# One exp in twenty-four moved from ScalarE to VectorE in a graph attention kernel

## The chip, the cores and the metric

The kernel runs on one core of a Trainium2 chip. The metric is the device time in microseconds of one launch, taken as the median of three runs. A core has five engines that run side by side, each through its own list of instructions in order: TensorE (PE, with its weight loads PEld), VectorE (DVE), ScalarE (ACT), GpSimd (POOL), and SyncE (SP), which here only issues DMAs. They wait for each other by semaphores.

## The reference

Four layers on a graph of N = 3327 nodes with 128 features, x of shape (3327, 128) and a dense fp32 matrix adj of (3327, 3327). Nearly all time goes into layer 0, an attention with 128 heads of only 8 features, whose logits get adj added twice:

```python
q = (x @ Wq.T).reshape(d, n, h)      # d = 128 heads, n = 3327, h = 8; k and v alike
a = jnp.einsum('dnh,dmh->dnm', q, k) * scale
a = a + spatial_encoding + edge_encoding          # both are adj
a = jax.nn.softmax(a, axis=2)
out = jnp.einsum('dnm,dmh->dnh', a, v).reshape(n, h * d)
return out @ Wo.T
```

Each of the four layers ends as x = layernorm(x + layer(x, adj)). Layers 1 to 3 are products of adj, or its transpose, with 128 columns. The attention needs 128 x 3327 x 3327, some 1.4 billion, exps.

## The kernel before

A prologue makes q, k and v, splits q and k into a high and a low part in fp32r, and writes them to scratch tensors in HBM (`q_s`, `k_s`, `v_img`). Then `attention()` runs, then the four layers' remaining products. There is also a path for large logits, `wide_attention()`, that these inputs don't take.

**Blocks, groups, sets.** The attention loop goes over 28 blocks: seven pieces of CW = 476 query columns times four ranges of keys (KBS), two of seven 128-key tiles and two of six. In a block it goes through 128 heads in 32 groups of GROUP = 4. For each head, `exponents(b, d, si)` works on three sets of tiles, one after the other: 3, 2 and 2 tiles where the block has seven, 2, 2 and 2 where it has six (`SETS`). For a set, TensorE adds this head's q·k to PSUM (L544): the PSUM tiles `sc` keep running logits, adj included, from head to head. That is possible since the keys hold the previous head's rows beside this head's, with negated queries, so that one product takes the old head's logits away and adds the new ones. A tile uses 64 of TensorE's rows, and tiles alternate between its two halves of rows, so two run side by side. Then one ScalarE instruction takes the exp of the whole set, from `sc` to `e` in SBUF (L548). There is one `sc` per set: the logits of a set for the next head wait until the exp of this set has been read. So TensorE can be at most two exps ahead.

**Weighs.** The exps of a group are multiplied with its values one group later. `weigh(b, g, r)` does it for one key tile and the four heads, four matmuls side by side into PSUM bank `o` (L562); a group has as many weighs as tiles, seven or six. [...] Three groups (PACK) share `o`: the first weigh of a pack restarts the bank, and after the last weigh of a pack, or of a block, `flush` adds the bank into `acc` on VectorE (L572, L574).

**The order.** Within the loop the order of TensorE, ScalarE, GpSimd and VectorE instructions is that of the program (`manual_schedule`). A group has 12 places, one after each set of each head; `PLACES` says after which places a weigh is issued:

```python
PLACES = {7: (1, 2, 4, 6, 7, 9, 11), 6: (1, 3, 5, 7, 9, 11)}
```

**Loads and side work.** At the first head of group n, `prepare` has SP load keys and queries for group n+2 (`load_heads`, L426 and L431, three buffers) and the values of group n+1 (`load_values`, L478), which GpSimd spreads into `v_pad` (L481). At the second head VectorE copies the keys of group n+1 one head on (`copy_keys`, L458 and L460), at the third it makes the negated and doubled queries (`copy_queries`, L466, L468, L469), at the fourth it does one step of `background_work`: adj is transposed and its row and column sums are taken in 78 pieces, spread over the groups (`PACE`), for the later layers; GpSimd issues the pieces' stores (L217).

## Time and profile before

| What | us |
|---|---|
| Median of three runs (11,215.2 to 11,219.94) | 11,218.06 |
| The profiled execution, its own time | 11,220.65 |
| Its span, first to last instruction | 11,218.9 |
| PE busy | 10,904.3 (97%) |
| ScalarE busy | 10,122.0 (90%) |
| VectorE busy | 5,422.6 (48%) |
| GpSimd busy | 1,712.0 (15%) |
| Exps on ScalarE (L548), 10,752 of them | 9,933.0 |
| VectorE's key copies (L458, L460) | 652.7 + 1,706.2 |
| VectorE's query copies (L466, L468, L469) | 807.9 + 353.8 + 1,034.9 |

The profile is one execution recorded by the hardware. A row of a group of instructions gives its line in the kernel, engine, operation, what it writes and reads, the count, the busy time with the mean ns of one, and the idle time of the engine just before with what ended it ("<-"). In the order in time, a row begins with the start and the length in us. A record of one instruction can overlap with the next of the same engine, so that records can be longer than the pace at which they follow; and a busy PE may be one whose records wait.

### The profile page before, as it was taken

The page shows a single profiled execution, that of the slowest core. Times are in us where ns is not written, and L with a number is a line of the kernel's source. Part 1 is how long each engine was busy: PE and PEld are TensorE (multiplying, and loading weights), DVE is VectorE, ACT ScalarE, POOL GpSimd, SP SyncE. Part 2 cuts the span into 40 slices and gives each one's busy share as a digit, 9 for nine tenths or more (in the row PEclk, how much of TensorE's full clock was granted, in tenths as well). Part 3 has the DMA queues.
Part 4 walks back from the last instruction along what each step waited for, and adds up shares of the span by engine and source line. Part 5 has one row for each costly group of instructions (what it writes and reads, how often), then busy time and mean ns, then how long its engine had stood idle before and what let it go on. Part 6 is the DMA issues. An engine that isn't in the chain of part 4 may idle for free. (4 is left out here: it accounts for less than half of the span.)

```text
span 11218.9 us, 197557 instructions
## 1 busy us (share of the span) xinstructions
PE 10904.3 (97%) x76607; PEld 3924.3 (35%) x76607; DVE 5422.6 (48%) x7864; ACT 10122.0 (90%) x11194; POOL 1712.0 (15%) x2738
## 2 busy tenths in 40 slices
PE   6699999999999999999999999999999999999999
PEld 2233333333333333333333333333333333333779
DVE  6444555445554455544555445554444544444312
ACT  2499999999999999999999999999999999999400
POOL 3311112111221111211112111121110100001200
PEclk8799999999999999999999999999999999999999
DMA  8655555555655556555556555555555555555686
GB/s 290 172 82 82 87 93 94 78 86 87 92 95 79 85 88 91 96 78 86 86 91 97 79 87 83 85 86 81 81 78 78 78 79 75 74 74 78 186 284 246
DMA packets 769475, 1157.40 MB, mean 103 GB/s; under 512 B 152703, under 2 KB 636401, under 8 KB 754201
## 3 DMA queue, kind: packets, MB, share of 16 engines
q1 hardware_dynamic: 673994, 913.64, 51.0%
q0 software_dynamic: 82432, 128.80, 4.4%
q10 hardware_dynamic: 12110, 102.22, 2.6%
q8 instruction: 616, 10.09, 0.5%
q14 instruction: 323, 2.65, 0.1%
HBM read 999.98 MB, written 143.98 MB: 102 GB/s over the span
## 5 line engine op out<-in xcount | busy, mean ns | idle before, releaser
L548 ACT ACTIVATE e<-sc 128x952 f32<-128x952 f32 (+1 forms) x10752 | 9933.0, 1350 | 93.9 <-PE sc L544 70.1
L562 PE MATMUL o<-e,v_pad 128*32 128x476 f32 (+1 forms) x46592 | 5867.7, 575 | 15.0 <-DVE acc L574 1.6
L544 PE MATMUL sc<-qt,kt 64*128 64x476 f32 x23296 | 4789.2, 458 | 58.0 <-DVE qt L468 3.8
L544 PEld LDWEIGHTS sc<-qt,kt 64*128 64x128 f32 x23296 | 2172.3, 183 | 5252.0 <-ACT e L548 5174.1
L460 DVE CAST kt<-kt 32x1152 fp32r<-32x1152 f32 (+1 forms) x1792 | 1706.2, 952 | 1358.2 <-DMA kt<-k_s 1352.2
L481 POOL COPY v_pad<-vs 128x192 f32<-128x192 f32 (+1 forms) x896 | 439.1, 490 | 8402.8 <-DMA vs<-v_img 6324.9
L562 PEld LDWEIGHTS o<-e,v_pad 128*32 128x32 f32 (+1 forms) x46592 | 922.8, 108 | 1538.9 <-issue 1536.1
L574 DVE TENSOR_TENSOR acc<-o,acc 128x476 f32<-128x476 f32 x231 | 151.0, 654 | 2373.6 <-PE o L562 2373.6
L469 DVE CAST qt<-qt 64x1904 fp32r<-64x1904 f32 x896 | 1034.9, 1155 | 30.5
L217 POOL DMA_DIRECT2D adjT_s<-at x1352 | 816.5, 612 | 213.4 <-DMA adjT_s<-at 77.6
L466 DVE TENSOR_SCALAR qt<-qt 32x1428 fp32r<-32x1428 f32 x896 | 807.9, 902 | 12.5
L458 DVE CAST kt<-kt 32x512 fp32r<-32x512 f32 (+1 forms) x1736 | 652.7, 376 | 38.2 <-PE sc L544 2.8
L572 DVE COPY acc<-o 128x476 f32<-128x476 f32 x77 | 50.3, 654 | 934.6 <-PE o L562 934.6
L1001 PE MATMUL bank<-y,eT 128*128 128x128 f32 (+1 forms) x4056 | 473.9, 276 | 0.4 <-DVE h L1123 0.4
L1001 PEld LDWEIGHTS bank<-y,eT 128*128 128x128 f32 (+1 forms) x4056 | 465.3, 192 | 5.7 <-DVE h L1123 0.6
L468 DVE TENSOR_SCALAR qt<-qt 32x476 fp32r<-32x476 f32 x896 | 353.8, 395 | 0.9
L966 ACT ACTIVATE rstd<-mv,eps 128x1 f32<-128x1 f32 x104 | 30.6, 295 | 302.5 <-DVE mv L964 291.5
L581 POOL DMA_DIRECT2D o_s<-acc x308 | 283.8, 926 | 41.4 <-DVE acc L574 23.6
L323 ACT ACTIVATE hi<-pp 128x1024 fp32r<-128x1024 f32 x52 | 52.8, 1025 | 178.5 <-PE pp L274 150.1
L274 PE MATMUL pp<-wqT,xT 128*128 128x512 f32 x104 | 61.7, 727 | 87.6 <-DVE lo L324 87.1
L1104 PE MATMUL bank<-a,y 128*128 128x512 f32 (+2 forms) x364 | 145.5, 562 | 0.0
L439 DVE MEMSET qt<- 32x476 f32 x28 | 12.7, 455 | 261.3 <-PE sc L544 260.4
(143 smaller groups left out, 1954.8 us busy)
## 6 DMA issues: line engine op xcount, KB each, us to landing
kt<-k_s SPq DMA_DIRECT2D x2688, 96.0 KB
kt<-k_s SPq DMA_DIRECT2D x896, 128.0 KB
qt<-q_s SPq DMA_DIRECT2D x896, 119.0 KB
qt<-q_s SPq DMA_DIRECT2D x1792, 59.5 KB
eT<-adjT_s SPq DMA_DIRECT2D x39, 1664.0 KB
eT<-adjT_s ACTq DMA_DIRECT2D x39, 1664.0 KB
vs<-v_img SPq DMA_DIRECT2D x448, 112.0 KB
adjT_s<-at POOLq DMA_DIRECT2D x1352, 32.0 KB, 3.8
```

Source lines behind the costliest of these rows:

```text
L217: nc.gpsimd.dma_start(out=flat_ap(adjT_s, (t * P + 32 * q) * NP + c * PIECE, [[NP, 32], [P, ns], [1, P]]), in_=at[32 * i:32 * i + 32].rear ...
L458: nc.vector.tensor_copy(kt[64 * rg + 32:64 * rg + 64, 0, 0:ns[rg] * P], heads[b, g - 1][0].bitcast(F32)[64 * rg:64 * rg + 32, GROUP - 1, 0 ...
L460: nc.vector.tensor_copy(kt[64 * rg + 32:64 * rg + 64, 1:, 0:ns[rg] * P], kf[64 * rg:64 * rg + 32, 0:GROUP - 1, 0:ns[rg] * P])
L466: nc.vector.tensor_scalar(qt[32:64, 1:], qf[0:32, 0:GROUP - 1], -1.0, None, ALU.mult)
L468: nc.vector.tensor_scalar(qt[32:64, 0], before, -1.0, None, ALU.mult)
L469: nc.vector.tensor_copy(qt[64:128], qf[0:64])
L481: nc.gpsimd.tensor_copy(vp[:, 32:32 + nt * GROUP * 32].rearrange("p (x c) -> p x c", c=32)[:, :, 0:H], vs[:, 0:nt * 32].rearrange("p (x c) ...
L544: nc.tensor.matmul(s[:, i, 0:CW], lhsT=kt[64 * rg:64 * rg + 64, k, pos * P:(pos + 1) * P], rhs=qt[64 * rg:64 * rg + 64, k, :], start=False ...
L548: nc.scalar.activation(e[:, 0:n, :], s[:, 0:n, 0:CW], AF.Exp, scale=2.0)
L562: nc.tensor.matmul(o[32 * j:32 * j + 32, 0:CW], lhsT=values[b, g][:m, c:c + 32], rhs=es[b, g * GROUP + j, r][:m, :], start=(r == 0 and u = ...
L581: nc.gpsimd.dma_start(out=flat_ap(o_s, blocks[b][0] + (f * PACK * GROUP + j) * N, [[GROUP * N, nb], [SLOTS, A1], [1, CW]]), in_=acc[32 * j ...
L1001: nc.tensor.matmul(ps[:n, 0:D], lhsT=e[:m, s, :n], rhs=y[:m, s, col:col + D], start=(s == 0), stop=(s == T - 1))
```

## The change

In every second group (those with even number), the exp of the third set of the group's first head is no longer a ScalarE instruction. `vector_exp` computes it on VectorE from nine instructions on 128x952 elements. The first one reads `sc` and so frees it; the other eight stand in a list `vec`, from which the loop emits one ahead of each following place. The polynomial gives the exp times a constant, so all other exps get the matching `bias=shift`, a [128,1] tile, where they had none. The lines below are those of the changed kernel.

Further: VectorE's key copies are gone, and the keys are loaded a second time into the rows that they filled. The values are loaded once for two groups. The places of the weighs differ between groups of odd and even number (in each pair, the first tuple is that of odd groups), and two weighs may share a place. The side work on adj has one buffer in place of two (`pe2`), a period of 8 groups in place of 9, and is done in two bursts, at groups 3 and 5 of the period.

```diff
-PACE = 9
+PACE = 8
+SHIFT = 6.625
+POLY = (-7.292605475782272, 41.836134677209586, -181.05570822282746, 522.4277799178005, -753.7042669615115)
+ROUND = 1.5 * 2 ** 23 + 127 + 256
...
+    shift = const.tile([P, 1], F32, name="shift")
+    nc.gpsimd.memset(shift, SHIFT)
...
-                tc.tile_pool(name="pe2", bufs=2) as pe, \
+                tc.tile_pool(name="pe2", bufs=1) as pe, \
...
-            PLACES = {7: (1, 2, 4, 6, 7, 9, 11), 6: (1, 3, 5, 7, 9, 11)}
+            PLACES = {7: ((0, 2, 4, 4, 7, 7, 9), (0, 0, 4, 7, 7, 9, 10)),
+                      6: ((0, 2, 4, 5, 7, 9), (0, 0, 3, 6, 8, 10))}
...
-                for rg in range(2):
-                    for u in range(2):
-                        row = 64 * rg + 16 * u
-                        nc.sync.dma_start(
-                            out=kf[row:row + 16, :, 0:ns[rg] * P],
-                            in_=flat_ap(k_s, d * N + (k0 + (ns[0] if rg else 0)) * P,
-                                        [[RS, 16], [N, GROUP], [1, ns[rg] * P]]))
+                for back in range(2):
+                    j = 1 if back and g == 0 else 0
+                    for rg in range(2):
+                        for u in range(2):
+                            row = 64 * rg + 32 * back + 16 * u
+                            nc.sync.dma_start(
+                                out=kf[row:row + 16, j:, 0:ns[rg] * P],
+                                in_=flat_ap(k_s, (d + j - back) * N + (k0 + (ns[0] if rg else 0)) * P,
+                                            [[RS, 16], [N, GROUP - j], [1, ns[rg] * P]]))
...
-            def copy_keys(b, g):
...
-                vs = kq.tile([P, 7 * 32], F32, name="vs")
-                nc.sync.dma_start(out=vs[:, 0:nt * 32],
-                                  in_=flat_ap(v_img, k0 * HD + g * nt * 32, [[T * HD, P], [1, nt * 32]]))
+                if g % 2 == 0:
+                    pairs[b, g // 2] = kq.tile([P, 2, 7 * 32], F32, name="vs", bufs=2)
+                    nc.sync.dma_start(out=pairs[b, g // 2].rearrange("p a c -> p (a c)")[:, 0:2 * nt * 32],
+                                      in_=flat_ap(v_img, k0 * HD + g * nt * 32, [[T * HD, P], [1, 2 * nt * 32]]))
+                vs = pairs[b, g // 2].rearrange("p a c -> p (a c)")[:, g % 2 * nt * 32:(g % 2 + 1) * nt * 32]
...
                     worked.append((u, c, next(steps)))
+                    next(steps)
                     turning.append(steps)
-                elif turning:
-                    if next(turning[0], None) is None:
-                        turning.pop()
+                if n % PACE == 5 and turning:
+                    for _ in turning.pop():
+                        pass
...
-                elif n + 1 < len(groups):
-                    if d % GROUP == 1:
-                        copy_keys(*groups[n + 1])
-                    elif d % GROUP == 2:
-                        copy_queries(*groups[n + 1])
-                    else:
-                        background_work(n)
+                elif d % GROUP == 2 and n + 1 < len(groups):
+                    copy_queries(*groups[n + 1])
+                elif d % GROUP == 3:
+                    background_work(n)
+
+            vec = []
+
+            def vector_exp(e, x):
+                y = ex.tile([P, 2, CW], F32, name="ey")
+                t = ex.tile([P, 2, CW], F32, name="et")
+                ti = t.bitcast(I32)
+                nc.vector.tensor_scalar(y, x, -63 * math.log(2.0), 2 / math.log(2.0), ALU.max, ALU.mult)
+                vec.append(lambda: nc.vector.tensor_scalar(t, y, ROUND, None, ALU.add))
+                vec.append(lambda: nc.vector.scalar_tensor_tensor(y, t, ROUND, y, ALU.subtract, ALU.subtract))
+                vec.append(lambda: nc.vector.tensor_scalar(ti, ti, 23, None, ALU.logical_shift_left))
+                for i, a in enumerate(POLY):
+                    vec.append(lambda i=i, a=a: nc.vector.scalar_tensor_tensor(
+                        e, e if i else y, a, t if i == len(POLY) - 1 else y, ALU.add, ALU.mult))
...
-                nc.scalar.activation(e[:, 0:n, :], s[:, 0:n, 0:CW], AF.Exp, scale=2.0)
+                if (b * NHG + d // GROUP) % 2 == 0 and (d % GROUP, si) == (0, 2):
+                    vector_exp(e[:, 0:n, :], s[:, 0:n, 0:CW])
+                else:
+                    nc.scalar.activation(e[:, 0:n, :], s[:, 0:n, 0:CW], AF.Exp, bias=shift, scale=2.0)
...
-                copy_keys(*groups[0])
...
+                        if vec:
+                            vec.pop(0)()
                         exponents(b, d, si)
-                        if queue and place in PLACES[len(queue_of)]:
+                        for _ in range(PLACES[len(queue_of)][d // GROUP % 2 == 0].count(place) if queue else 0):
                             weigh(*queue.pop(0))
```

## The prediction

> **What bounds the kernel now.** I read the busy time by stretches of the span first, then the costliest groups, then the order in time. From 433 to 10,435 us the attention loop runs; ScalarE is never idle in it:

> ```profile
> 2000.00:4000.00 2000.00, 1984.88 (x14140) 633.79 (x14137) 1005.12 (x1388) 1987.41 (x2111) 328.60 (x550) 1.00 0.57 86
> ```

> The columns after the length are PE, PE's weight loads, VectorE, ScalarE (1987.41 of 2000), GpSimd, TensorE clock, DMA share. PE looks as full, but its records contain waiting; the groups say who waits:

> ```profile
> L548 ACT ACTIVATE e<-sc 128x952 f32<-128x952 f32 (+1 forms) x10752 | 9933.0, 1350 | 93.9 <-PE sc L544 70.1
> L544 PEld LDWEIGHTS sc<-qt,kt 64*128 64x128 f32 x23296 | 2172.3, 183 | 5252.0 <-ACT e L548 5174.1
> L574 DVE TENSOR_TENSOR acc<-o,acc 128x476 f32<-128x476 f32 x231 | 151.0, 654 | 2373.6 <-PE o L562 2373.6
> ```

> The exps (L548) idle 93.9 us in all; the logits' weight loads wait 5174 us for them. VectorE (48% busy) waits for PE, so its work is worth nothing by itself. The pace is read where the queries of each group are loaded, in a block of seven and one of six tiles:

> ```profile
> 5007.29 1.02 SPq L426 DMA_DIRECT2D qt<-q_s  x3
> 5019.19 1.02 SPq L426 DMA_DIRECT2D qt<-q_s  x3
> ...
> 5601.41 1.02 SPq L426 DMA_DIRECT2D qt<-q_s  x3
> 5611.70 1.02 SPq L426 DMA_DIRECT2D qt<-q_s  x3
> ```

> So a group of 12 exps takes 11.90 or 10.29 us: 0.857 us for an exp of 952, 1.26 for one of 1428 (eight and four of them in the first). PE is close behind:

> ```profile
> 5002.49 0.16 PEld L562 LDWEIGHTS o<-e,v_pad 128*32 128x32 f32 x8 [0.33 <-issue]
> 5003.43 0.19 PEld L544 LDWEIGHTS sc<-qt,kt 64*128 64x128 f32 x2 [0.78 <-ACT e L548]
> 5003.84 0.16 PEld L562 LDWEIGHTS o<-e,v_pad 128*32 128x32 f32 x8 [0.23 <-issue]
> ```

> From start to start a weigh takes PE 0.94 us and the logits of two tiles 0.41; three tiles, which need a second round through the two row halves, I take as 0.63. So PE could be little faster than ScalarE, and what stops PE for more than its lead of two exps stops ScalarE.

> [...] The exps before have none; after, every one has `bias=shift`. [...] with the same shape from PSUM with and without a pointer:

> ```profile
> L1044 ACT ACTIVATE y<-bank,dinv 128x128 f32<-128x128 f32 x25 | 9.3, 374 | 4.4 <-PE bank L986 4.4
> L1055 ACT COPY y<-bank 128x128 f32<-128x128 f32 x25 | 6.7, 267 | 60.4 <-DVE x L1054 60.4
> ```

> Does it stay when they follow each other? [...] a copy without a pointer hands over after 0.15 us, L1044 after 0.26.

> ```profile
> 10501.78 0.25 ACT L978 COPY xT<-bank 128x128 f32<-128x128 f32 x1
> 10501.93 0.37 ACT L1044 ACTIVATE y<-bank,dinv 128x128 f32<-128x128 f32 x1
> 10502.19 1.07 ACT L1027 COPY oT<-bank 128x512 f32<-128x512 f32 x2
> ```

> [...] L1084 has both in SBUF, L1123 one in PSUM.

> ```profile
> L466 DVE TENSOR_SCALAR qt<-qt 32x1428 fp32r<-32x1428 f32 x896 | 807.9, 902 | 12.5
> L324 DVE SCALAR_TENSOR_TENSOR lo<-pp,hi 128x1024 fp32r<-128x1024 f32 x52 | 62.7, 1218 | 30.6 <-ACT hi L323 26.4 <-DMA q_s<-lo 4.0
> L1084 DVE SCALAR_TENSOR_TENSOR h<-z,dinv,x 128x128 f32<-128x128 f32 x25 | 8.8, 352 | 0.9
> L1123 DVE SCALAR_TENSOR_TENSOR h<-bank,inv_row,z 128x128 f32<-128x128 f32 x25 | 8.8, 351 | 39.3 <-PE bank L1001 39.3
> ```

> **The change part by part.**
> *Exps taken from ScalarE:* 448 (one in each even group of 28 blocks x 16) x 0.857 = -384 us, all of it on the path that sets the end.
> *Bias pointer:* 10,304 exps left; [...] 0.116 (0.262 - 0.146 above), taken 0.10: +1030. The pace becomes 0.957 and 1.36.
> *The polynomial:* nine VectorE instructions on 128x952. From the rows [...]: 1.15 (PSUM) + 0.65 + 1.15 + 0.65 + 5 x 1.15 = 9.36 us. Each but one waits for the one before, and such a wait leaves a gap instead of an overlap:

> ```profile
> 5023.38 0.90 DVE L466 TENSOR_SCALAR qt<-qt 32x1428 fp32r<-32x1428 f32 x1
> 5024.20 0.39 DVE L468 TENSOR_SCALAR qt<-qt 32x476 fp32r<-32x476 f32 x1
> 5024.63 1.15 DVE L469 CAST qt<-qt 64x1904 fp32r<-64x1904 f32 x1
> ```

> L468 starts 0.08 before L466 ends, L469 (it waits for L468) 0.04 after. So 9.6 us; the query copies (5023.38 to 5025.78: 2.4) stand among them by program order. The total (VectorE about 5423 - 2359 + 4193 = 7256 us) has room.
> *What is queued behind it:* in an even group the weigh of place 10 is the last; if it ends a pack of three groups, `flush` follows on VectorE behind all nine. The next odd group's weigh at place 0 restarts bank `o` and waits for that flush; the logits of set 1 stand behind it on PE, and ScalarE behind those. Six times in a block (five packs and the block's last), 168 times in all. This is worked out on a clock with T0 = start of the even group's first exp, for seven tiles / six. Its queue is then: the group's first logits start at -1.5 (two exps ahead, less the 0.4 by which a record, 1.31 us for 952 elements in the groups by form, outlasts the pace), two weighs at place 0 end at +1.0 / +0.8, the logits of set 1 are ready at 1.45 / 1.3 (0.48 for one pair), where ScalarE wants it at 1.36 / 0.96 (bubble 0.1 / 0.3), the first VectorE operation starts at 1.7 / 1.5. Plus 9.6 + 2.4 + 0.7: flush ends at 14.4 / 14.2. The even group has 11 exps: the next starts at 12.25 / 10.8, so that PE wants to weigh at 11.35 / 9.7 (as the even group's weighs at -0.9 / -1.1) and waits 3.0 / 4.5; the odd group's first exp ends at 13.6 / 11.8. The odd group's set 1 is ready 1.5 us after the flush (weigh 0.94, logits 0.48, hand-over): 15.9 / 15.7. ScalarE idles 2.3 / 3.9, mean 3.1 x 168 = +520. Before, the flush at place 11 met an idle VectorE (L562's row on the page has PE waiting 1.6 us for L574 in all).
> *Bubble in even groups:* 224 x (0.1 + 0.3) = 90 at most, 0 at least if PE regains it; taken 45.
> *At nothing:* key copies gone (L460, L458: 2359 us, all beside ScalarE). Key loads doubled: eight issues for four, 1.7 us more on SP, which then idles about 9 us a group; the keys' share of the DMA time (382 of 914 MB of a queue at 51%: 21 points) comes twice, 0.58 to about 0.8, still hidden, as loads go out two groups (over 20 us) ahead; if late, the first logits of a group wait. Set 2's logits now wait for VectorE's first operation (1.15 us), but are wanted three places later. One value load for two: half the packets, GpSimd's copies as before. Single piece buffers, PACE 8: loads at 0, last reading at 5, stores at 6 of 8 groups; 78 x 8 = 624 of 896 groups. Its bursts on VectorE (two operations of 1.22 us) fall at the last head of odd groups, where no polynomial runs.
> Sum: -384 + 1030 + 520 + 45 = +1211 on the profiled 11,220.65, which is 2.6 above the median of three runs: **12,430 us**. Own range: bias -72/+165, chain 5% either way 100, bubble 45: 12,210 to 12,740.

> **Rivals.** (A) *The bias is read under the exp before.* For it: records of L548 overlap deeply (1.31 at a pace of 0.86). Against: L1044. Groups are then shorter and the flush later against them: ScalarE idles 3.4 / 5.0, 168 x 4.2 = 706, bubbles 110: -384 + 816 = +432, 11,650. (B) *The flush is ready in time*, because VectorE is quicker or PE later: -384 + 1030 + 45: 11,910. It decides from a chain 3 to 4.5 us shorter; the rows that price it (1.15 and 0.65 us) speak against that. (C) *ScalarE stays the only pace and an exp in 24 is gone*: place L548, price -384, bubbles 110 back: 10,945, faster. It decides if what is added to ScalarE's stream stays under 384/10,304 = 37 ns an exp and the flush under 384/168 = 2.3 us together; for it, ScalarE's idle 93.9 us; against, both numbers above. That the exps don't move is excluded by the program order.

> **Chances.** Main 0.72, A 0.11, B 0.09, C 0.08 (0.02 of it within 0.2%, about what a measurement of this kernel can tell from no change). Range 11,620 to 12,700: it leaves out C and the tails. Faster 0.06, same 0.02, slower 0.92.

> **What would show it.** L548's pace 0.95 in six-tile groups with a `shift` operand (0.86: A); the weighs' idle time put down to VectorE's `acc`, some 168 times and 3 to 4.5 us each (none: B); VectorE's polynomial rows 1.15 and 0.65 us; no wait of the logits for key loads. A shorter span would refute both terms at once.

## The result and the profile after

| | before | after |
|---|---|---|
| median, us | 11,217.0 | 12,624.1 (12,618.2 to 12,627.7) |
| ratio to before | | 1.1254, interval 1.1234 to 1.1273 |
| profiled span, us | 11,218.9 | 12,616.4 |
| first to last exp, us | 10,001.9 | 11,400.5 |

The kernel became slower by 12.5%, 1407 us. Of these, 1399 lie between the first and the last exp, so the stages around the attention loop can be left alone.

The costliest groups of instructions of the kernel after (count, then busy time and mean ns of one, then the engine's idle time ahead of them and what ended most of it):

```profile
L565 ACT ACTIVATE e<-sc,shift 128x952 f32<-128x952 f32 (+1 forms) x10304 | 10523.7, 1176 | 902.9 <-PE sc L558 862.1
L579 PE MATMUL o<-e,v_pad 128*32 128x476 f32 (+1 forms) x46592 | 5845.9, 592 | 671.3 <-DVE acc L591 529.7
L558 PEld LDWEIGHTS sc<-qt,kt 64*128 64x128 f32 x23296 | 2296.6, 188 | 5420.6 <-ACT e L565 4053.0
L534 DVE TENSOR_SCALAR ey<-sc 128x952 f32<-128x952 f32 x448 | 515.2, 1150 | 3744.2 <-PE sc L558 2144.5
L539 DVE SCALAR_TENSOR_TENSOR e<-e,ey 128x952 f32<-128x952 f32 x1344 | 1545.7, 1150 | 46.2
L535 DVE TENSOR_SCALAR et<-ey 128x952 f32<-128x952 f32 x448 | 294.8, 658 | 15.4
L591 DVE TENSOR_TENSOR acc<-o,acc 128x476 f32<-128x476 f32 x231 | 150.1, 650 | 320.5 <-PE o L579 320.5
```

Two readings. First, there are 448 exps fewer (10,304), yet they are busy for 591 us more than before: each one got dearer, and its operands now list `shift`. (The mean of one record fell, from 1350 to 1176 ns, since the records overlap less: those of 952 elements take 1309 ns at a pace of 857 before, 1107 at 945 after; the mean is not the pace.) Second, the exps' own idle time rose from 93.9 to 902.9 us, and the chain of blame can be followed through the rows: the exps wait for the logits (`sc`), and the weighs (L579), which stand ahead of those logits on TensorE, wait 529.7 us for VectorE's flush (`acc`). Before, the weighs hardly waited:

```profile
L562 PE MATMUL o<-e,v_pad 128*32 128x476 f32 (+1 forms) x46592 | 5867.7, 575 | 15.0 <-DVE acc L574 1.6
```

The flush itself (L591) waits little for the weighs that fill its bank, 320.5 us where it was 2373.6: it is late because of what stands ahead of it on VectorE.

The order in time of the kernel after, the query loads in a block of six tiles, one at the start of each group:

```profile
5005.34 1.02 SPq L436 DMA_DIRECT2D qt<-q_s  x3
5016.32 1.02 SPq L436 DMA_DIRECT2D qt<-q_s  x3
5033.19 1.02 SPq L436 DMA_DIRECT2D qt<-q_s  x3
5044.17 1.02 SPq L436 DMA_DIRECT2D qt<-q_s  x3
5055.10 1.02 SPq L436 DMA_DIRECT2D qt<-q_s  x3
```

An even and an odd group together take 21.91 us where no flush lies between them (5033.19 to 5055.10) and 27.85 where one does (5005.34 to 5033.19). Before, two such groups took 20.58. So there is a loss in every group and a second one, three to five times as large for a pair, at each flush. The second is seen in the order in time around the flush at 5020.88 (start, length, engine, operation, and in brackets the wait before it and who ended it):

```profile
5016.26 3.52 DVE L539 SCALAR_TENSOR_TENSOR e<-e,ey 128x952 f32<-128x952 f32 x3
5019.81 1.15 DVE L539 SCALAR_TENSOR_TENSOR e<-e,et 128x952 f32<-128x952 f32 x1
5020.88 0.65 DVE L591 TENSOR_TENSOR acc<-o,acc 128x476 f32<-128x476 f32 x1
5021.67 1.81 PE L579 MATMUL o<-e,v_pad 128*32 128x476 f32 x8 [4.67 <-DVE acc L591]
5023.41 0.50 PEld L558 LDWEIGHTS sc<-qt,kt 64*128 64x128 f32 x4 [1.54 <-issue]
5024.22 2.00 ACT L565 ACTIVATE e<-sc,shift 128x952 f32<-128x952 f32 x2 [5.10 <-PE sc L558]
5024.50 1.76 PE L579 MATMUL o<-e,v_pad 128*32 128x476 f32 x8
5026.77 1.05 ACT L565 ACTIVATE e<-sc,shift 128x952 f32<-128x952 f32 x1 [0.55 <-PE sc L558]
```

The last four instructions of the polynomial run, then the flush, then at once the weigh that had waited 4.67 us for it, then the logits, then the exp, which had waited 5.10 us. One thing in these lines was in no step of the forecast: this weigh takes about 1.7 us to the start of the next work on TensorE, and so does the one after it, where one took 0.94 before. The busy time by stretches around it (start and end, length, PE, its weight loads, VectorE, ScalarE, GpSimd, granted TensorE clock, DMA share, GB/s) says why:

```profile
5016.60:5018.90 2.30, 0.40 (x2) 0.10 (x1) 2.23 (x3) 2.30 (x3) 1.18 (x3) 1.00 0.67 163
5018.90:5025.70 6.80, 4.03 (x20) 0.93 (x20) 4.95 (x6) 1.70 (x3) 0.00 (x0) 0.53 1.11 134
5025.70:5032.00 6.30, 6.30 (x50) 1.73 (x46) 0.00 (x0) 5.75 (x7) 2.74 (x5) 0.97 0.22 47
```

TensorE stops near 5017.0; about 2 us later its granted clock drops to about half, for 6.8 us, through the rest of the wait and past its end. Counted through the loop, its first 50 us left out, there are 167 such stretches (82 of 3.4 us, 85 of 6.8), 860 us in all, where the kernel before has none.

With these the 1399 us can be laid out from the trace of the kernel after:

- exps gone from ScalarE: 448 x 0.857 = -384
- pace of the exps, end to end where they follow each other: 0.857 to 0.945 us for 952 elements, 1.254 to 1.342 for 1428: 0.088 x 10,304 = +907
- flush: what the odd groups behind a flush take beyond that pace, summed over their exps, on average 3.93 us with seven tiles and 5.97 with six (84 groups of each kind): +832
- bubble at the second exp of even groups with six tiles, 1.122 for 0.945: 224 x 0.177 = +40

The sum is +1395; 4 us are left.

### The profile page after: what moved, and what is told of

It is laid out like the page before. It is cut to its first block, busy times and chain, and to the rows that moved or that the text cites. A ratio compares the mean times of both kernels' runs of the same rounds, so it can differ in the third digit from the quotient of the medians.

```text
span 12616.4 us, 201203 instructions
## 1 busy us (share of the span) xinstructions
PE 11183.5 (89%) x76607; PEld 4176.4 (33%) x76607; DVE 7316.9 (58%) x8368; ACT 10713.5 (85%) x10746; POOL 1451.0 (12%) x2739
## 5 line engine op out<-in xcount | busy, mean ns | idle before, releaser
L565 ACT ACTIVATE e<-sc,shift 128x952 f32<-128x952 f32 (+1 forms) x10304 | 10523.7, 1176 | 902.9 <-PE sc L558 862.1
L579 PE MATMUL o<-e,v_pad 128*32 128x476 f32 (+1 forms) x46592 | 5845.9, 592 | 671.3 <-DVE acc L591 529.7
L558 PE MATMUL sc<-qt,kt 64*128 64x476 f32 x23296 | 4933.8, 455 | 502.2 <-ACT e L565 264.1
L534 DVE TENSOR_SCALAR ey<-sc 128x952 f32<-128x952 f32 x448 | 515.2, 1150 | 3744.2 <-PE sc L558 2144.5
L579 PEld LDWEIGHTS o<-e,v_pad 128*32 128x32 f32 (+1 forms) x46592 | 1050.3, 110 | 2513.4 <-issue 2425.4
L539 DVE SCALAR_TENSOR_TENSOR e<-e,ey 128x952 f32<-128x952 f32 x1344 | 1545.7, 1150 | 46.2
L468 DVE CAST qt<-qt 64x1904 fp32r<-64x1904 f32 x896 | 1030.4, 1150 | 30.5
L536 DVE SCALAR_TENSOR_TENSOR ey<-et,ey 128x952 f32<-128x952 f32 x448 | 515.7, 1151 | 15.5
L539 DVE SCALAR_TENSOR_TENSOR e<-e,et 128x952 f32<-128x952 f32 x448 | 515.2, 1150 | 15.4
L539 DVE SCALAR_TENSOR_TENSOR e<-ey 128x952 f32<-128x952 f32 x448 | 515.5, 1151 | 13.9
L591 DVE TENSOR_TENSOR acc<-o,acc 128x476 f32<-128x476 f32 x231 | 150.1, 650 | 320.5 <-PE o L579 320.5
L535 DVE TENSOR_SCALAR et<-ey 128x952 f32<-128x952 f32 x448 | 294.8, 658 | 15.4
L537 DVE TENSOR_SCALAR et<-et 128x952 int32<-128x952 int32 x448 | 294.3, 657 | 15.4
L984 ACT ACTIVATE rstd<-mv,eps 128x1 f32<-128x1 f32 x104 | 30.6, 295 | 294.5 <-DVE mv L982 277.4
```

Of the source, the lines that this page charges most:

```text
L468: nc.vector.tensor_copy(qt[64:128], qf[0:64])
L534: nc.vector.tensor_scalar(y, x, -63 * math.log(2.0), 2 / math.log(2.0), ALU.max, ALU.mult)
L536: vec.append(lambda: nc.vector.scalar_tensor_tensor(y, t, ROUND, y, ALU.subtract, ALU.subtract))
L539: vec.append(lambda i=i, a=a: nc.vector.scalar_tensor_tensor(e, e if i else y, a, t if i == len(POLY) - 1 else y, ALU.add, ALU.mult))
L558: nc.tensor.matmul(s[:, i, 0:CW], lhsT=kt[64 * rg:64 * rg + 64, k, pos * P:(pos + 1) * P], rhs=qt[64 * rg:64 * rg + 64, k, :], start=False ...
L565: nc.scalar.activation(e[:, 0:n, :], s[:, 0:n, 0:CW], AF.Exp, bias=shift, scale=2.0)
```

## The experiments

The theory taken into them was: two separate losses, the pointer operand in every exp, and the flush that stands behind the polynomial. The rivals were that the doubled loads or VectorE's traffic slow the exps, that the flush's cost is only its wait, and that the flush costs nothing of its own. The ratio in each line is to the kernel before, with its interval; that kernel's median in these comparisons is 11,220 us (11,217 in the last).

**The pointer alone**, put into the kernel before:

```diff
+    shift = const.tile([P, 1], F32, name="shift")
+    nc.gpsimd.memset(shift, 0.0)
...
-                nc.scalar.activation(e[:, 0:n, :], s[:, 0:n, 0:CW], AF.Exp, scale=2.0)
+                nc.scalar.activation(e[:, 0:n, :], s[:, 0:n, 0:CW], AF.Exp, bias=shift, scale=2.0)
```

> The kernel before with one change: every exp gets a [128,1] bias tile that holds zeros, so that the values stay the same. If the bias pointer is what lengthened the exps' pace from 0.857 to 0.945 us (the change's trace), all 10,752 exps cost 0.088 us more: +946, about 12,165 us, and the pace of a six-tile group becomes 0.945. If instead the pace was lengthened by the doubled key loads or by VectorE's traffic, neither of which is here, the time stays at 11,220.

Measured: 12,148.2 us, ratio 1.0828 (1.081 to 1.0846), +928. Its row among the groups, and two query loads in a block of six tiles from the order in time:

```profile
L550 ACT ACTIVATE e<-sc,shift 128x952 f32<-128x952 f32 (+1 forms) x10752 | 10874.3, 1686 | 78.7 <-PE sc L546 77.7
```

```profile
6063.70 1.02 SPq L428 DMA_DIRECT2D qt<-q_s  x3
6075.05 1.02 SPq L428 DMA_DIRECT2D qt<-q_s  x3
```

ScalarE waits for nothing more than before (78.7 us idle), and a group of twelve exps takes 11.35 us where it took 10.29. So 928 / 10,752 = 0.086 us for each exp, with no new load and no VectorE work in the kernel. Rival A of the prediction, the bias read under the exp before, is refuted.

**The pointer taken out of the kernel after**, an immediate of the same value in its place:

```diff
-                    nc.scalar.activation(e[:, 0:n, :], s[:, 0:n, 0:CW], AF.Exp, bias=shift, scale=2.0)
+                    nc.scalar.activation(e[:, 0:n, :], s[:, 0:n, 0:CW], AF.Exp, bias=SHIFT, scale=2.0)
```

> The changed kernel with the bias as an immediate number instead of a pointer. Pointer theory: the pace returns to 0.857, -907 us for 10,304 exps; the groups become 1 us shorter while VectorE's chain stays, so that each of 168 waits for the flush grows by some 0.9 us (+150) and the bubbles by some 70: about 11,940. If the pace comes from the loads or VectorE: unchanged, 12,620.

Measured: 12,115.8 us, ratio 1.0798 (1.078 to 1.0816). That is 508 less than after, not the 684 expected. The pace is back at 0.857 and 1.254. What is missing is in the groups of the flush:

```profile
L565 ACT ACTIVATE e<-sc 128x952 f32<-128x952 f32 (+1 forms) x10304 | 9669.5, 1066 | 1250.6 <-PE sc L558 1242.7
L579 PE MATMUL o<-e,v_pad 128*32 128x476 f32 (+1 forms) x46592 | 5885.4, 596 | 759.3 <-DVE acc L591 599.6
```

Faster exps finish the even group sooner, while the flush is no earlier: the exps' idle time goes from 902.9 to 1250.6 us. The odd groups behind a flush now lose 5.82 (seven tiles) and 7.45 us (six) on average, 84 x 5.82 + 84 x 7.45 = 1115 where it was 832; the stretches at half clock grow from 860 to 1062 us. The expectation had added 150 for the longer wait and 70 for the bubbles. The trace shows 283 for the flush, half clock included, and about 98 for the bubbles in even groups, which are now 0.13 and 0.51 us. The two losses are not independent: removing one makes the other dearer.

**The flush ahead of the last five instructions of the polynomial**, in the even groups that end with one; nothing else is touched:

```diff
-                        if vec:
+                        if vec and not (len(vec) <= 5 and d // GROUP % 2 == 0 and place < 11 and queue
+                                        and (queue_of[0][1] % PACK == PACK - 1 or queue_of[0][1] == NHG - 1)):
                             vec.pop(0)()
```

> The changed kernel (bias pointer and all), but in the even groups in which a flush comes, the last five of the nine polynomial instructions are issued behind the flush, at the following five places. If the 168 long pairs of groups (28.7 and 27.8 us instead of 24.9 and 21.9) come from the flush standing behind the polynomial, nearly all of 817 us goes: about 11,810, and no wait of the weighs for acc is left. If they come from something else in those groups (the bank's restart, loads), the time stays near 12,620.

Measured: 11,798.7 us, ratio 1.0516 (1.0499 to 1.0534): 825 less than after, where the trace had put 832 down to the flush. The weighs' row:

```profile
L579 PE MATMUL o<-e,v_pad 128*32 128x476 f32 (+1 forms) x46592 | 5634.0, 573 | 4.9 <-POOL v_pad L482 2.2
```

Their idle time falls from 671.3 to 4.9 us, pairs of groups take 24.9 or 21.9 us with and without a flush, and no stretch at half clock is left in the loop after its first 50 us. The polynomial still has its nine instructions and VectorE its load; only the place of the flush in VectorE's order is another. So that place is the cause of this loss, and the polynomial's time on VectorE costs nothing by itself. Rival B is refuted too.

**Wait or clock?** TensorE is kept busy while the weigh waits, by products of zeros that are added to the running logits of set 1, which leaves them as they are:

```diff
+    zeros = const.tile([P, 512], F32, name="zeros")
+    nc.gpsimd.memset(zeros, 0.0)
...
                         exponents(b, d, si)
+                        if place == 0 and queue and d // GROUP % 2 and queue_of[0][1] % PACK == 0:
+                            for _ in range(3 if KBS[blocks[b][1]][1] == 7 else 5):
+                                nc.tensor.matmul(sc[1][:, 0, 0:CW], lhsT=zeros[:, 0:P], rhs=zeros[:, 0:CW],
+                                                 start=False, stop=True, skip_group_check=True)
```

> The changed kernel; in the odd groups whose first weigh waits for the flush, TensorE first adds products of zeros to set 1's logits (3 matmuls of 128x476 fp32 in seven-tile blocks, 5 in six-tile ones[...]), so that it works during most of the wait and the values stay as they are. In the changed kernel's trace the granted clock falls to half for 3.4 or 6.8 us in each such wait, and the weigh after it takes 1.8 us instead of 0.94. If TensorE's standing still causes that, the waits keep their 3.4 and 4.7 us but the slow stretch behind them goes: some 84 x 1.5 + 84 x 2 = 290 us less, about 12,330, with a granted clock near 0.985 instead of 0.955. If the clock falls for another reason (load, temperature), the time stays at 12,620 or grows with the added work.

Measured: 12,347.2 us, ratio 1.1003 (1.0985 to 1.1021): 277 less than after, with more work on TensorE. The clock view of after and then of this kernel:

```profile
core 0: 12616.4 us, clock 0.955
```

```profile
core 0: 12335.6 us, clock 0.989
```

No half-clock stretch is left in the loop after its first 50 us, and the weigh starts 0.15 us after the end of the flush, as it did, so the products don't hold it up. The odd groups behind a flush now lose 2.43 (seven tiles) and 4.16 us (six) on average: 84 x 2.43 + 84 x 4.16 = 554 us of wait. The other 832 - 554 = 278 us were the slow clock, as the measured time, 277 less, says. Both parts are real, two thirds wait and one third clock.

**How short a wait still costs clock?** As the hold of five, with only the last two instructions held back, `len(vec) <= 2`:

```diff
-                        if vec and not (len(vec) <= 5 and d // GROUP % 2 == 0 and place < 11 and queue
+                        if vec and not (len(vec) <= 2 and d // GROUP % 2 == 0 and place < 11 and queue
```

> The changed kernel with only the last two of the nine polynomial instructions (2 x 1.18 us) behind the flush in the groups in which one comes. If the loss is the wait alone, each of 168 flush pairs gets 2.4 us shorter: -400, about 12,220. If a short standstill also spares TensorE the half clock, seven-tile pairs lose nearly all of their 3.8 us and six-tile ones about 4 of 5.9: -640, about 11,980. The run with all five behind the flush gave 11,799, which is the floor.

Measured: 12,092.9 us, ratio 1.0776 (1.0758 to 1.0794), 531 less than after and between the two figures expected. With seven tiles nearly the whole loss is gone (0.17 us a flush is left), with six 3.44 us are left.

```profile
L579 PE MATMUL o<-e,v_pad 128*32 128x476 f32 (+1 forms) x46592 | 5739.8, 582 | 274.6 <-DVE acc L591 233.7
```

With seven tiles TensorE's wait itself is gone, save in the first groups of a block. With six it still waits for the flush, 2.3 us in the median and at most 2.8, and still 89 stretches at half clock remain (84 of them with six tiles, where there are 84 such waits; 68 are of 3.4 us), 375 us in all. Neither expectation was right: so short a wait does not spare the clock.

The traces show more closely when the clock falls. The starts of the stretches lie on one grid: in each kernel they are whole multiples of 3.413 us apart, and nearly all stretches are one or two such steps long. In the step just ahead of a fall, TensorE's matmul records fill at most 0.51 of the time in the kernel after (0.56 in this one, 0.50 in the one with the immediate); in steps at full clock that no fall follows, at least 0.59 (0.67, 0.53). The clock is back after a step that they fill to at least 0.90. What goes with a fall in these traces is a step in which TensorE is busy for no more than about half of the time (0.56 at most), and not how long it has stood: in the kernel after, the fall comes between 1.6 and 4.8 us after TensorE stopped, as the wait happens to lie on the grid.

**The loads alone**: the kernel after without polynomial and bias and with the weighs' places of before, so that only the key loads, the value loads for two groups, the single buffers and the later background work are left of the change:

```diff
-            PLACES = {7: ((0, 2, 4, 4, 7, 7, 9), (0, 0, 4, 7, 7, 9, 10)),
-                      6: ((0, 2, 4, 5, 7, 9), (0, 0, 3, 6, 8, 10))}
+            PLACES = {7: ((1, 2, 4, 6, 7, 9, 11),) * 2, 6: ((1, 3, 5, 7, 9, 11),) * 2}
...
-                if (b * NHG + d // GROUP) % 2 == 0 and (d % GROUP, si) == (0, 2):
+                if False:
...
-                    nc.scalar.activation(e[:, 0:n, :], s[:, 0:n, 0:CW], AF.Exp, bias=shift, scale=2.0)
+                    nc.scalar.activation(e[:, 0:n, :], s[:, 0:n, 0:CW], AF.Exp, scale=2.0)
```

> Only the parts that were costed at nothing: key loads in place of VectorE's copies, values loaded for two groups, one buffer and period 8 for the work on adj. All exps stay on ScalarE without a bias, the places are those of before. If these parts are off the path: 11,220 within 0.3%. If the doubled key loads come late or disturb ScalarE's writes, it is slower, and the logits show waits for k_s.

Measured: 11,226.8 us, ratio 1.0006 (0.9997 to 1.0015): no difference. The busy time in the stretch that the prediction showed of before, columns as above:

```profile
2000.00:4000.00 2000.00, 1984.94 (x14144) 633.81 (x14136) 567.93 (x711) 1987.35 (x2112) 313.20 (x591) 1.00 0.86 125
```

VectorE falls from 1005 to 568 us in 2000 and the DMA share rises from 0.57 to 0.86, and ScalarE is as full as before (1987.35 us against 1987.41). All of this part of the change costs nothing, and gains nothing by itself.

**Both losses removed**: the immediate and the hold of five together.

> The changed kernel with both: immediate bias, and the five instructions behind the flush. If the two terms are the whole loss, what is left is 448 exps x 0.857 = -384 against before, less bubbles of some 100 us: about 10,940, faster than before. If PE is the bound once ScalarE is relieved, or the key loads cost something, it stays near 11,200.

Measured: 11,037.3 us, ratio 0.984 (0.9823 to 0.9856): faster than the kernel before, by 183 us or 1.6%. The rows of the exps and the weighs:

```profile
L565 ACT ACTIVATE e<-sc 128x952 f32<-128x952 f32 (+1 forms) x10304 | 9626.9, 1069 | 210.8 <-PE sc L558 209.2
L579 PE MATMUL o<-e,v_pad 128*32 128x476 f32 (+1 forms) x46592 | 5637.2, 573 | 17.5 <-POOL v_pad L482 13.9
```

Pointer and flush together are worth 12,624 - 11,037 = 1587 us, more than 508 + 825 one by one, as the interaction above asks. The figure expected is missed by 97 us. The exps' idle time, 210.8 us, is for logits again, but now most of it in the even groups, mainly at the second exp: they lose 0.13 us with seven tiles and 0.52 with six, the first of each block left out, 136 us in all.

**Can the bubbles be taken back by other places for the weighs?** Two tries on top of that kernel; the second changes only blocks of six tiles.

```diff
-            PLACES = {7: ((0, 2, 4, 4, 7, 7, 9), (0, 0, 4, 7, 7, 9, 10)),
-                      6: ((0, 2, 4, 5, 7, 9), (0, 0, 3, 6, 8, 10))}
+            PLACES = {7: ((0, 2, 4, 4, 7, 7, 9), (0, 1, 4, 7, 7, 9, 10)),
+                      6: ((1, 2, 5, 7, 9, 10), (0, 1, 6, 7, 9, 10))}
```

> The run with immediate bias and the flush ahead (11,037), with other places: in even groups the second weigh is issued after set 1 instead of two after set 0, and in six-tile blocks the odd groups' first weigh at place 1. Its remaining loss against -384 is the second exp of an even group, which follows after 1.30 instead of 0.857 us in six-tile and 0.935 in seven-tile blocks. If two weighs in a row before set 1's logits cause that, some 224 x (0.5 + 0.1) = 130 us go: about 10,900. If ScalarE's wait for its own set's release causes it, nothing changes.

```diff
-                      6: ((0, 2, 4, 5, 7, 9), (0, 0, 3, 6, 8, 10))}
+                      6: ((0, 2, 4, 5, 7, 9), (0, 3, 5, 6, 8, 10))}
```

> The run with immediate bias and the flush ahead (11,037), with one other tuple of places: six-tile even groups weigh at (0, 3, 5, 6, 8, 10) instead of (0, 0, 3, 6, 8, 10). There the second exp of the group follows after 1.30 instead of 0.857 us, and moving the second weigh behind set 1's logits only moved the gap to the third exp (1.44). If the gap is TensorE's total work before the third exp's logits (two weighs and four sets in the time of two exps), taking one weigh out of that stretch closes most of it: up to 224 x 0.5 = 110 us less, about 10,930. If TensorE has no room later in the group either, the gap comes back there and the time stays within 0.5% of 11,037.

Measured: 11,207.5 us, ratio 0.9989 (0.9982 to 0.9995), and 11,062.9 us, ratio 0.9862 (0.9845 to 0.9878). Both missed what was hoped. In the first, the gap only moved to the third exp (end to end 1.51 us for a pace of 1.254 with seven tiles, 1.44 for 0.857 with six) and new ones came at later places; pairs with six tiles take 20.8 to 21.1 us where they took 20.23. In the second it came back at the fourth and seventh exps (1.18 and 1.21 us), and pairs take 20.4 to 20.5. Of the three orders tried, none closes the gap. A likely reason is that with a pace of 0.857 TensorE has hardly any slack in a group that has one exp less and the same weighs; that it is TensorE's total work, and not these three orders, was not shown.

## Why the prediction was right, and where its sizes were off

- **Direction and the two places** were right, and the time lies in the range. The forecast of 12,430 is 194 below the 12,624 measured.
- **Exps taken from ScalarE, -384:** as worked out; counts and pace agree.
- **Bias pointer, +1030: too large.** The runs show 0.088 us an exp in the kernel after (907 in all) and 0.086 alone. The step took 0.10, an estimate of the author's. What the trace of before shows for it is one pair of 128x128 instructions, whose hand-overs are 0.116 us apart and which differ in their operation too (ACTIVATE and COPY). In the long stream of exps a little less than that stays in the pace.
- **Polynomial on VectorE:** the rows are the ones worked out, 1150 and 658 ns for the forecast's 1.15 and 0.65. In one group the chain with the query copies ran from 4965.12 to 4977.17, 12.05 us, where the step had 9.6 + 2.4 = 12.0. VectorE's total is 7316.9 us for 7256. The 1.15 and 0.65 follow, to within 0.01, from rows of before: L574 (654 ns for 476 elements) and L324 (1218 for 1024) give 1.03 ns an element and 0.16 us besides, 1.14 us for 952; L466 (902 for 1428) and L468 (395 for 476) give 0.53 and 0.14, 0.65 us. L539 with both sources in SBUF took 1150 ns for 952 elements, as L534 did with its source in PSUM.
- **Flush, +520: mis-sized, measured 832.** This is the step that failed, and mainly one term of it. The clock from T0 gave ScalarE 2.3 and 3.9 us of idleness at each flush; the kernel with TensorE kept busy shows 2.43 and 4.16, and the weigh in the lines above waits 4.67 for the 4.5 forecast. What the step had wrong is that it gave the weigh and the logits behind the flush their normal times: 0.94 us for the weigh and 0.48 for the logits of two tiles. They ran at half clock, which is 278 us in all. (In the trace of before the two matmuls of such a set, 458 ns each on the mean, run side by side: at 5003.43 us they take 0.48 together. A set of three tiles takes 0.62, from 5001.87 to 5002.49; the eight matmuls of a weigh, 575 ns each, take 1.00 from there.) In the kernel after, the clock is 0.5 in every record of these stretches, and they last 3.4 or 6.8 us. TensorE did not have to stand for a whole step of 3.413 us: waits of at most 2.8 us were enough with the hold of two, and the clock fell after steps in which TensorE was busy for up to 0.56 of the time. The forecast had no term for this.
- **Bubble in even groups, +45:** 40, nearly all with six tiles.
- **At nothing:** confirmed by the kernel with the loads alone. The DMA share is 0.86 there, 0.77 in the same stretch of the kernel after, for the 0.8 forecast.
- **Rivals:** A falls by the pointer alone, B by the hold of five. C, ScalarE the only pace with an exp in 24 gone, needs both losses away. The kernel without them stands at 11,037 for its 10,945, so the gain that the change was able to bring is there and is half as large as 384: of the missing 200 us, 136 are the bubbles, and most of the rest lies in small gaps of the odd groups (some 30) and in the first groups of the blocks (some 20).
- **Luck.** The errors of the two terms have opposite signs (-123 and +312), and each is larger than the prediction had allowed for that term (-72 for the bias, 100 for the flush). That the total lies in the range is in part luck.

## What to carry to other kernels

Price each operand of an instruction that paces the kernel by its count: a bias that is a pointer cost 0.086 us here, 928 us in 10,752 exps, and the same number as an immediate cost nothing. When work goes to an engine off the critical path, look at what stands behind it in that engine's order and releases a single buffer: nine instructions with room to spare cost 832 us because one short flush came after them, and holding back five gave all of it back. Take such losses away together before judging the idea: with the pointer gone alone, the flush cost 283 us more.
